# Cross-attention chain: the second attention written as one list of every engine's pieces, in place of a loop and a drain

## The chip, the cores and the metric

One core of one Trainium2 chip runs the kernel as a single program. The metric is device time in microseconds, the median of several executions. The engines are PE (matrix multiply), DVE (vector), ACT (scalar and activation), POOL (GpSimd) and SP, which only issues transfers. Each engine works through its own instructions in the order in which the program lists them, and waits in place when an instruction's data or buffer is not ready.

## The reference, cut to what matters

Thirty-two batches of 256 tokens with 256 features pass two layers:

```python
q, k, v = heads(tgt @ Wq.T), heads(mem @ Wk.T), heads(mem @ Wv.T)   # 16 heads
x = tgt + merge(softmax(q @ k.T / sqrt(dk)) @ v)[0]                 # batch 0's attention, added to all
norm_X   = layernorm(ctx, norm1_w, norm1_b)                         # memory
norm_F_L = layernorm(x, norm2_w, norm2_b)                           # queries
attended = softmax(norm_F_L @ norm_X.T * scale) @ norm_X            # first attention, per batch
h        = gelu(attended @ fc1_w.T + fc1_b)                         # 4 hidden values per token
cross    = h @ fc2_w.T + fc2_b
norm_c   = layernorm(cross, norm3_w, norm3_b)
self_att = softmax(norm_c @ norm_c.T * scale) @ norm_c              # second attention, per batch
out      = norm_F_L + gamma2 * (cross + gamma1 * self_att)
```

Only four hidden values per token enter `cross`, so the kernel never builds the 256-wide rows of the second attention. A token is a slot of at most 32 numbers: `v_sl` holds the four hidden values, a one, and later the weighted sums; `u_sl` and `t_sl` hold the normalised coefficients and their product with a small Gram matrix. Scores of the second attention are products over 32 rows.

## The kernel before, in words

The scheduler is off: the order of calls in the source is the order of the instructions on each engine, and buffers are handed out in that order.

Work is cut into 32 steps of one batch for the first attention (`first_step(s)`), in groups of four batches, g = 0 to 7. Groups of the second attention run behind, the first two already between the steps; the change begins where the steps end, at step 32. Steps 32 to 35 only finish the first attention of the last group.

For each group g the second attention consists of these pieces. A pair p is two batches; group g has the pairs 2g and 2g + 1.

- `third(k)`, for the two groups 2k and 2k + 1: a chain that alternates between POOL and DVE. `third_a` is a Gram product on POOL (L997), `third_b` a sum on DVE (L1007) and a product on POOL (L1009), `third_c` a sum on DVE (L1015), then on POOL a scaling, a power, a product and a second Gram product (L1017, L1019, L1022, L997), `third_d` a sum on DVE into `t_sl` (L1026). Ahead of `third(3)` stand `hide` (three small DVE operations) and `activate` (gelu on ACT).
- `turn_u(g)`: four transposes on PE and a copy of `u_sl` and `t_sl`; `turn_t(g)`: two transposes and a copy of `t_sl`; `turn_v(g)`: two and a copy of `v_sl`.
- A product by queries (pair p; `by_queries`) gives scores whose row maxima DVE takes (`scores_max`, L1153). A product by keys (`by_keys`) gives the transposed scores less the maxima, of which ACT takes the exponential (`weights`, L1165). `self_values(g)` sums over keys on PE (L354, named pu) and copies; `self_weighted(g)` transposes the sum (L1079); `divide(g)` divides on DVE (L1084, L1085) and writes `v_sl`. A product `to_output` (pair p) is added on DVE to `x_all` (`output`, L1175 for single banks, L1178 for a pair of banks), and SP stores 512 KB (L1179).
- `scale_skip(n)`: POOL multiplies batch n of `x_all` by a weight row (L764). The add of pair p needs batches 2p and 2p + 1 scaled. Batches 0 to 11 are scaled during the steps.

`pair_products` (L439) issues the eight products of 32 rows of each pair it is given. Two pairs, one even and one odd, use different row groups of PE, and their instructions are interleaved, two of the one and two of the other. The product of one pair needs two PSUM banks. There are three such places: `s0` and `s1`, each one buffer of two banks, and `et`, two buffers of one bank. Transposes and sums over keys use two buffers called `tp`.

In before a loop over j = 3 to 7 issues, in each round: the transposes of group j - 1, a pair block of queries 2j with keys 2j - 3, a block of output 2j - 6 with queries 2j + 1, the sums of group j - 2, a block of keys 2j - 2 with output 2j - 5, the division of group j - 2 and three or four scales. Behind it stands a drain of 42 lines for the last groups. Maxima use `s0`, keys use `s1`, outputs use `et`, until the drain.

Of the kernel before, what the change touches and what calls it, by code (L numbers as in the profile page):

```python
# [27 lines left out]
def tile_xattn_seq(  # L28
# [51 lines left out]
    def bank(tag, name):  # L80
        return ps.tile([P, NC, D], F32, tag=tag, name=name)
# [263 lines left out]
        copy(nxT_of[q][:, b], pt)  # L345

    def by_columns(psum, name, weights, moving, copy=nc.vector.tensor_copy, by_pairs=False):

        pg = psum(f"p{name}")
        order = [(kc, b) for kc in range(NC) for b in range(QB)]  # L350
        if by_pairs:
            order.sort(key=lambda at: at[1] // 2)
        for kc, b in order:
            nc.tensor.matmul(  # L354
                pg[SL * b : SL * (b + 1), 0, :],
                weights(kc, b),
                moving[:, b, kc, :],
                start=(kc == 0),
                stop=(kc == NC - 1),
            )  # L360
        t = wk.tile([P, D], F32, tag="col", name=f"col_{name}", bufs=3)
        copy(t, pg[:, 0, :])
        return t
# [639 lines left out]
        third[k] = times_gram(rows_of(k)[0], gram_m, NM, f"m{k}")  # L1003

    def third_b(k):
        vg = small.tile([P, TG, NM], F32, tag="vg3", name=f"vg3_{k}", bufs=2)
        nc.vector.tensor_reduce(vg, third.pop(k), AX.X, ALU.add)  # L1007
        vgv = small.tile([P, TG, NM], F32, tag="vgv3", name=f"vgv3_{k}", bufs=2)
        nc.gpsimd.tensor_mul(vgv, vg, rows_of(k)[0])  # L1009
        third[k] = vgv  # L1010

    def third_c(k):
        v5, u6, _ = rows_of(k)
        var = small.tile([P, TG], F32, tag="var3", name=f"var3_{k}", bufs=2)
        nc.vector.tensor_reduce(var, third.pop(k), AX.X, ALU.add)  # L1015
        ve = small.tile([P, TG], F32, tag="ve3", name=f"ve3_{k}", bufs=2)
        nc.gpsimd.tensor_scalar(ve, var, 0.0, EPS, ALU.max, ALU.add)  # L1017
        r3 = small.tile([P, TG, 1], F32, tag="r3", name=f"r3_{k}", bufs=2)
        nc.gpsimd.tensor_tensor(  # L1019
            r3.rearrange("p t o -> p (t o)"), ve, neg_half[:, 0:TG], ALU.pow  # L1020
        )
        nc.gpsimd.tensor_mul(u6[:, :, 0:NM], v5, r3.to_broadcast([P, TG, NM]))  # L1022
        third[k] = times_gram(u6, gram_k, NK, f"k{k}")
# [12 lines left out]
            )  # L1036

    def turn_u(g, copy=nc.scalar.copy):
        pt = bank("tp", f"pt_u{g}")
        slots_first(pt[:, 0, :], u_sl[:, g])  # L1040
        slots_first(pt[:, 1, :], t_sl[:, g])
        ut_of[g] = late.tile([P, NC, D], F32, tag="ut", name=f"ut_{g}", bufs=3)
        copy(ut_of[g], pt)

    def turn(what, sl, g, copy=nc.scalar.copy):

        pt = bank("tp", f"pt_{what}{g}")
        slots_first(pt[:, 0, :], sl[:, g])
        vt_of[what, g] = late.tile([P, D], F32, tag=f"{what}t", name=f"{what}t_{g}", bufs=2)
        copy(vt_of[what, g], pt[:, 0, :])  # L1050

    def turn_v(g, copy=nc.scalar.copy):
        turn("v", v_sl, g, copy)

    def turn_t(g, copy=nc.scalar.copy):
        turn("t", t_sl, g, copy)

    def by_queries(p, dst):
        ut = ut_of[p // 2]
# [8 lines left out]
    def self_values(g):  # L1068

        pvt_of[g] = by_columns(  # L1070
            tp_bank, f"u{g}", lambda kt, b: u_sl[:, g, kt, b, :], eT_of.pop(NQ + g), nc.scalar.copy
        )

    def self_weighted(g):

# [69 lines left out]
    ps2 = ctx.enter_context(tc.tile_pool(name="ps2", bufs=1, space=PSUM, reuse_waits="tile"))  # L1145

    def pair_bank(tag, name):
        t = ps2.tile([P, 2, NC, D], F32, tag=tag, name=name)
        return t, [t[:, i] for i in range(2)]

    def scores_max(p, sc):
        b = p % 2 * 2
        nc.vector.tensor_reduce(  # L1153
            t_sl[:, p // 2, :, b : b + 2, NK].rearrange("p t b -> p b t"),
            sc,
            AX.X,
            ALU.max,
            negate=True,
        )

    def weights(p, sc):
        if p % 2 == 0:
            eT_of[NQ + p // 2] = ld.tile([P, QB, NC, D], F32, tag="cq", name=f"eT2_{p // 2}")
        b = p % 2 * 2
        nc.scalar.activation(eT_of[NQ + p // 2][:, b : b + 2], sc, AF.Exp)  # L1165

    def out_banks(p):
        return [bank("et", f"po_{p}_{i}") for i in range(2)]

    def output(p, po):  # L1170

        if isinstance(po, list):
            for i in range(2):
                n = 2 * p + i
                nc.vector.tensor_add(x_all[:, n], po[i], x_all[:, n])  # L1175
        else:
            xs = x_all[:, 2 * p : 2 * p + 2]
            nc.vector.tensor_add(xs, po, xs)  # L1178
        nc.sync.dma_start(by_tokens(out[2 * p : 2 * p + 2]), x_all[:, 2 * p : 2 * p + 2])  # L1179


    first_step(B)
    sc, banks = pair_bank("s1", "sc1_2")
    pair_products(by_keys(2, banks))
    first_step(B + 1)
    weights(2, sc)
    pa = self_weighted(0)
    divide(0, pa)
    first_step(B + 2)
    third_d(2)  # L1190

    for j in range(3, NQ):


        turn_t(j - 1)
        if j == 3:
            turn_v(0, by_vector)
        sc0, b0 = pair_bank("s0", f"sc0_{2 * j}")
        sc1, b1 = pair_bank("s1", f"sc1_{2 * j - 3}")
        pair_products(by_queries(2 * j, b0), by_keys(2 * j - 3, b1))  # L1200
        scores_max(2 * j, sc0)
        if j > 3:
            turn_v(j - 3)
        weights(2 * j - 3, sc1)
        if j == 3:
            first_step(B + 3)
            hide(6, 8)
            activate(6)
            third_a(3)
        if j + 1 < NQ:  # L1210
            turn_u(j + 1)
        po = out_banks(2 * j - 6)
        sc0, b0 = pair_bank("s0", f"sc0_{2 * j + 1}")
        pair_products(to_output(2 * j - 6, po), by_queries(2 * j + 1, b0))
        if j < NQ - 1:
            output(2 * j - 6, po)
            scores_max(2 * j + 1, sc0)
        else:
            scores_max(2 * j + 1, sc0)
            output(2 * j - 6, po)  # L1220
        self_values(j - 2)
        if j == NQ - 1:
            break
        if j == 3:
            third_b(3)
        if j == 4:
            third_d(3)
        sc1, b1 = pair_bank("s1", f"sc1_{2 * j - 2}")
        po = out_banks(2 * j - 5)
        pair_products(by_keys(2 * j - 2, b1), to_output(2 * j - 5, po))  # L1230
        weights(2 * j - 2, sc1)
        pa = self_weighted(j - 2)
        output(2 * j - 5, po)
        divide(j - 2, pa)
        if j == 3:
            third_c(3)
        done = len(scaled_at) + max(3 * (j - 3), 4 * (j - 3) - 2)
        for n in range(done, min(done + (3 if j < 5 else 4), B)):
            scale_skip(n)
    for n in range(len(scaled_at) + 14, B):  # L1240
        scale_skip(n)


    g = NQ - 1
    sc1, b1 = pair_bank("s1", f"sc1_{2 * g - 2}")
    pair_products(by_keys(2 * g - 2, b1))
    weights(2 * g - 2, sc1)
    turn_t(g)
    sc0, b0 = pair_bank("s0", f"sc1_{2 * g - 1}")
    pair_products(by_keys(2 * g - 1, b0))  # L1250
    pa = self_weighted(g - 2)
    weights(2 * g - 1, sc0)
    divide(g - 2, pa)
    sc1, b1 = pair_bank("s1", f"sc1_{2 * g}")
    po = out_banks(2 * g - 5)
    pair_products(by_keys(2 * g, b1), to_output(2 * g - 5, po))
    output(2 * g - 5, po)
    turn_v(g - 2)
    weights(2 * g, sc1)
    self_values(g - 1)  # L1260
    sc0, b0 = pair_bank("s0", f"sc1_{2 * g + 1}")
    po = out_banks(2 * g - 4)
    pair_products(by_keys(2 * g + 1, b0), to_output(2 * g - 4, po))
    weights(2 * g + 1, sc0)
    pa = self_weighted(g - 1)
    divide(g - 1, pa)
    output(2 * g - 4, po)
    po1, b1 = pair_bank("s1", f"po_{2 * g - 3}")
    pair_products(to_output(2 * g - 3, b1))
    turn_v(g - 1)  # L1270
    output(2 * g - 3, po1)
    self_values(g)
    po = out_banks(2 * g - 2)
    po1, b1 = pair_bank("s0", f"po_{2 * g - 1}")
    pair_products(to_output(2 * g - 2, po), to_output(2 * g - 1, b1))
    pa = self_weighted(g)
    divide(g, pa)
    output(2 * g - 2, po)
    turn_v(g)
    output(2 * g - 1, po1)  # L1280
    po = out_banks(2 * g)
    po1, b1 = pair_bank("s1", f"po_{2 * g + 1}")
    pair_products(to_output(2 * g, po), to_output(2 * g + 1, b1))
    output(2 * g, po)
    output(2 * g + 1, po1)
# [1 line left out]
_INS = [  # L1287
    "x",
# [45 lines left out]
```

## Time and profile before

| what | value |
|---|---|
| median of 4 runs | 231.95 us (231.41 to 232.44) |
| profiled execution, its own time | 232.44 us |
| its span | 230.7 us |
| granted PE clock, mean | 0.985 |
| PE busy | 211.1 us, 92% |
| POOL busy | 174.5 us, 76% |
| DVE busy | 168.5 us, 73% |
| ACT busy | 148.3 us, 64% |
| bytes moved | 33.81 MB, of them 8.39 MB written |

Times in the profile run from the start of the span. The part that the change touches begins at about 173 us. A busy PE is a PE with at least one matrix multiply in flight by the profile's model, so a late start can hide inside busy time; the chain of waits, which splits time by what released what, shows it better. The page's list of the costliest groups gives the mean of one instruction; instructions that follow one another on an engine overlap a little, so that a run of them takes less than the sum of the means.

### The profile page before, as it was taken

The page shows a single profiled execution, that of the slowest core. Times are in us where ns is not written, and L with a number is a line of the kernel's source. Part 1 is how long each engine was busy: PE and PEld are TensorE (multiplying, and loading weights), DVE is VectorE, ACT ScalarE, POOL GpSimd, SP SyncE. Part 2 cuts the span into 40 slices and gives each one's busy share as a digit, 9 for nine tenths or more (in the row PEclk, how much of TensorE's full clock was granted, in tenths as well). Part 3 has the DMA queues.
Part 4 walks back from the last instruction along what each step waited for, and adds up shares of the span by engine and source line. Part 5 has one row for each costly group of instructions (what it writes and reads, how often), then busy time and mean ns, then how long its engine had stood idle before and what let it go on. Part 6 is the DMA issues. An engine that isn't in the chain of part 4 may idle for free.

```text
span 230.7 us, 4951 instructions
## 1 busy us (share of the span) xinstructions
PE 211.1 (92%) x1797; PEld 154.1 (67%) x1797; DVE 168.5 (73%) x409; ACT 148.3 (64%) x302; POOL 174.5 (76%) x274
## 2 busy tenths in 40 slices
PE   7999898898999989999998999989999998999950
PEld 6766555676787768697886887766775666655530
DVE  2797989899988748667677677686274977784681
ACT  2554968698988285966787968437846855545500
POOL 6067598576999999999978899997079479999300
PEclk9999999999999999999999999999999999999985
DMA  6889998999959964180730000000000224442277
GB/s 224 276 298 357 395 386 170 198 249 242 207 102 338 276 116 171 32 153 2 131 54 1 0 3 0 3 2 5 4 0 0 85 100 185 182 168 109 97 282 262
DMA packets 18038, 33.81 MB, mean 147 GB/s; under 512 B 1175, under 2 KB 2142, under 8 KB 18014
## 3 DMA queue, kind: packets, MB, share of 16 engines
q1 hardware_dynamic: 12974, 24.33, 29.5%
q0 software_dynamic: 3696, 7.34, 18.2%
q10 hardware_dynamic: 1344, 1.84, 2.3%
q8 instruction: 14, 0.23, 0.4%
q14 instruction: 10, 0.08, 0.1%
HBM read 17.73 MB, written 8.39 MB: 113 GB/s over the span
## 4 chain that ended last, share of the span: by engine, by line
PE 44%; POOL 23%; DVE 18%; DMA 4%; ACT 4%; issue 3%; DVEq 0%; POOLq 0%; ACTq 0%
PE sc L773 8%; PE sc L439 7%; POOL cq L307 6%; DMA x_all<-att 4%; POOL rs_b L227 4%; DVE st L211 4%; PE po L439 3%; PE pu L354 3%; POOL x_all L329 3%; DVE x_all L1175 2%; PE pt_e L202 2%; PE pv L354 2%; PE pt_x L202 2%; POOL rs_x L227 2%; PE ph L354 2%
## 5 line engine op out<-in xcount | busy, mean ns | idle before, releaser
L773 PE MATMUL sc<-nxT,nfT 128*128 128x256 f32 x256 | 62.4, 386 | 0.7 <-ACT nfT L755 0.7
L773 PEld LDWEIGHTS sc<-nxT,nfT 128*128 128x128 f32 x256 | 45.7, 190 | 12.1 <-issue 5.3
L764 POOL TENSOR_TENSOR x_all<-x_all,w_bc 128x512 f32<-128x512 f32 x32 | 39.7, 1286 | 0.0
L786 ACT ACTIVATE e<-sc,nm 128x256 f32<-128x256 f32 x64 | 26.9, 474 | 19.8 <-DVE nm L783 19.6
L783 DVE TENSOR_REDUCE nm<-sc 128x2 f32<-128x512 f32 x32 | 22.0, 687 | 22.1 <-PE sc L773 10.4
L755 ACT ACTIVATE nfT<-pt_x,bq,wq 128x256 f32<-128x256 f32 x64 | 33.3, 582 | 1.6 <-PE pt_x L202 1.5
L211 DVE BATCH_NORM_STATS2 st<-x_all 128x6 f32<-128x256 f32 x64 | 23.2, 412 | 1.8 <-DMA x_all<-att 1.7
L202 PE MATMUL pt_x<-ident,x_all 128*128 128x128 f32 x132 | 20.7, 278 | 1.5 <-POOL x_all L329 1.2
L202 PE MATMUL pt_c<-ident,cq 128*128 128x128 f32 x132 | 19.7, 276 | 2.2 <-ACT nfT L755 1.7
L211 DVE BATCH_NORM_STATS2 st<-cq 128x6 f32<-128x256 f32 x56 | 20.6, 412 | 0.0
L202 PE MATMUL pt_e<-ident,e 128*128 128x128 f32 x128 | 19.5, 275 | 0.6 <-ACT e L786 0.5
L1175 DVE TENSOR_TENSOR x_all<-po,x_all 128x512 f32<-128x512 f32 x26 | 16.7, 682 | 4.1 <-PE po L439 2.9
L307 POOL TENSOR_SCALAR cq<-cq,rs_b,nmr_b 128x256 f32<-128x256 f32 x32 | 19.4, 682 | 0.0
L795 ACT COPY eTq<-pt_e 128x512 f32<-128x512 f32 x32 | 18.5, 588 | 0.4 <-PE pt_e L202 0.4
L202 PEld LDWEIGHTS pt_x<-ident,x_all 128*128 128x128 f32 x132 | 15.4, 143 | 4.8 <-POOL x_all L329 2.4
L439 PE MATMUL po<-w_out,vt 32*128 32x256 f32 x128 | 17.5, 401 | 1.2 <-ACT vt L1050 1.0
L202 PEld LDWEIGHTS pt_e<-ident,e 128*128 128x128 f32 x128 | 15.4, 140 | 4.4 <-ACT e L786 1.6
L439 PE MATMUL sc<-tt,ut 32*128 32x256 f32 x128 | 17.6, 401 | 0.4 <-ACT eT L1165 0.4
L202 PEld LDWEIGHTS pt_c<-ident,cq 128*128 128x128 f32 x132 | 15.0, 141 | 3.9 <-ACT nfT L755 2.7
L1165 ACT ACTIVATE eT<-sc 128x1024 f32<-128x1024 f32 x14 | 14.4, 1027 | 4.6 <-PE sc L439 2.5
L345 DVE COPY nxT<-pt_c 128x512 f32<-128x512 f32 x23 | 15.6, 676 | 2.3 <-PE pt_c L202 2.3
L331 ACT ACTIVATE x_all<-x_all,nmr_b,rs_b 128x256 f32<-128x256 f32 x16 | 9.8, 618 | 10.9 <-POOL nmr_b L236 10.9
(215 smaller groups left out, 446.2 us busy)
## 6 DMA issues: line engine op xcount, KB each, us to landing
out_dram<-x_all SPq DMA_DIRECT2D x16, 512.0 KB
x_all<-att POOLq DMA_DIRECT2D x7, 1024.0 KB, 10.1
cq<-in_ctx_dram SPq DMA_DIRECT2D x6, 1024.0 KB
x_all<-in_x_dram SPq DMA_DIRECT2D x4, 1024.0 KB
x_all<-in_x_dram SPq DMA_DIRECT2D x1, 2048.0 KB
x_all<-in_x_dram SPq DMA_DIRECT2D x1, 1792.0 KB
cq<-in_ctx_dram ACTq DMA_DIRECT2D x1, 1024.0 KB
cq<-in_ctx_dram SPq DMA_DIRECT2D x1, 768.0 KB
```

Of the source, the lines that this page charges most:

```text
L202: nc.tensor.transpose(pt[:, dc, t * P : (t + 1) * P], src[:, t, dc * P : (dc + 1) * P], ident)
L211: nc.vector.bn_stats(st[:, t, :], src[:, t, :])
L307: nc.gpsimd.tensor_scalar(row, row, rs[:, i + t, :], nmr[:, i + t, :], ALU.mult, ALU.add)
L354: nc.tensor.matmul(pg[SL * b : SL * (b + 1), 0, :], weights(kc, b), moving[:, b, kc, :], start=(kc == 0), stop=(kc == NC - 1),)
L439: nc.tensor.matmul(dst[i][:, t, :], lhs[r : r + SL, t * P : (t + 1) * P], rhs[r : r + SL, :], start=True, stop=True,)
L755: nc.scalar.activation(nfT_of[n][:, dc, :], px[:, dc, :], AF.Identity, bias=bq[:, dc : dc + 1], scale=wq2[:, dc : dc + 1],)
L764: nc.gpsimd.tensor_mul(x_all[:, n], x_all[:, n], w2_bc.unsqueeze(1).to_broadcast([P, NC, D]))
L773: nc.tensor.matmul(sc[:, qt, :], nfT[:, dc, qt * P : (qt + 1) * P], nxT[:, dc, :], start=(dc == 0), stop=(dc == NC - 1),)
L783: nc.vector.tensor_reduce(nm, sc, AX.X, ALU.max, negate=True)
L786: nc.scalar.activation(e[:, qt, :], sc[:, qt, :], AF.Exp, bias=nm[:, qt : qt + 1])
L795: nc.scalar.copy(eT_of[q][:, b], turned(e_of.pop(n), "et", f"e_{n}"))
L1175: nc.vector.tensor_add(x_all[:, n], po[i], x_all[:, n])
```

## The change

The loop and the drain are replaced by one list of words, read from left to right. Each word is one engine's piece: transposes, their copy, a pair block, its maxima, exponentials or adds are words of their own, so that another piece can stand between a product and what drains it. Helpers are split for this (`by_columns` into `columns` and `copy_columns`, `turn_u` and `turn` into transposes and copy, `third_b` and `third_c` into their DVE and POOL halves).

A block names the place of each of its products (`q6@s1+q7@et`), so queries, keys and outputs may use any of `s0`, `s1` and `et`. In words: `q`, `k`, `o` products by queries, by keys and to the output; `max`, `exp`, `add` what drains them; `turn_x` transposes and `tT`, `uT`, `vT` their copies (`.v` on DVE, otherwise on ACT); `sums` and `col` the sums over keys and their copy; `turn_a` and `a` the transposes and the division; `pre`, `gelu`, `m`, `vg`, `vgv`, `var`, `r`, `t_k` the pieces of `third`; `scale` one scaling on POOL.

Keys of pair 3 are multiplied in one block with those of pair 2, between steps 33 and 34. All scales stand where the list puts them, from `scale12` on at its front. The copies of `turn_t` and `turn_v` have three buffers each instead of two. The pieces themselves and their sizes stay the same, except that a maximum or an exponential of a pair in `et` is two instructions of one bank, and an add of a pair in `s0` or `s1` one instruction of two banks.

```diff
-    def turn(what, sl, g, copy=nc.scalar.copy):
+    def turned_slots(what, g):
         pt = bank("tp", f"pt_{what}{g}")
-        slots_first(pt[:, 0, :], sl[:, g])
-        vt_of[what, g] = late.tile([P, D], F32, tag=f"{what}t", name=f"{what}t_{g}", bufs=2)
+        slots_first(pt[:, 0, :], {"v": v_sl, "t": t_sl}[what][:, g])
+        return pt
+
+    def copy_slots(what, g, pt, copy):
+        vt_of[what, g] = late.tile([P, D], F32, tag=f"{what}t", name=f"{what}t_{g}", bufs=3)
         copy(vt_of[what, g], pt[:, 0, :])
...
     def pair_bank(tag, name):
+        if tag == "et":
+            banks = [bank("et", f"{name}_{i}") for i in range(2)]
+            return banks, [(i, i + 1, banks[i].unsqueeze(1)) for i in range(2)]
         t = ps2.tile([P, 2, NC, D], F32, tag=tag, name=name)
-        return t, [t[:, i] for i in range(2)]
+        return [t[:, i] for i in range(2)], [(0, 2, t)]
...
+    def products(*todo):
+        by = {"q": by_queries, "k": by_keys, "o": to_output}
+        args = []
+        for what, p, tag in todo:
+            banks, held[what, p] = pair_bank(tag, f"{what}_{p}")
+            args.append(by[what](p, banks))
+        pair_products(*args)
...
     first_step(B)
-    sc, banks = pair_bank("s1", "sc1_2")
-    pair_products(by_keys(2, banks))
-    first_step(B + 1)
-    weights(2, sc)
     pa = self_weighted(0)
     divide(0, pa)
+    first_step(B + 1)
+    products(("k", 2, "s1"), ("k", 3, "s0"))
+    weights(2, held.pop(("k", 2)))
+    weights(3, held.pop(("k", 3)))
     first_step(B + 2)
-    third_d(2)
-
-    for j in range(3, NQ):
...
-    output(2 * g, po)
-    output(2 * g + 1, po1)
+    order = """
+    scale12 q6@s1+q7@et t_k2 turn_t2 max6 scale13 turn_u4 tT2 turn_n7 uT4.v k4@s0+k5@s1
+    scale14 n7 max7 sums1 exp4 scale15 turn_u5 exp5 col1.v q8@s0+q9@et pre6 scale16 uT5
+    gelu6 sums2 max8 scale17 max9 q11@s1+q10@s0 m3 max11 turn_t4 scale18 col2 tT4
+    turn_a2 turn_v0 vg3 k9@et+k8@s1 vT0 a2 vgv3 max10 scale19 turn_t3 exp9 turn_a1 var3
+    exp8 a1 r3 o1@s0+o0@et tT3.v turn_v1 add1 sums4 vT1 add0 turn_v2 col4 o3@s0+k6@s1
+    vT2 turn_a4 add3 exp6 k7@et scale20 a4 o4@s1+o5@s0 exp7 t_k3 scale21 turn_t5 add4
+    turn_u7 tT5 turn_u6 uT7 add5 scale22 uT6 q15@s1+k10@et scale23 q12@s0 max15 exp10
+    scale24 max12 q13@et+q14@s1 sums3 scale25 max13 turn_v4 col3 max14 scale26
+    o2@s0+k11@et vT4 turn_t6 add2 exp11 scale27 turn_t7 o9@s1 tT6 tT7 scale28 turn_a3
+    k14@s0+k15@et a3 add9 scale29 turn_v3 exp15 sums5 vT3.v scale30 exp14 o7@et+k12@s1
+    col5.v scale31 turn_a5 add7 exp12 sums7 o6@s1+k13@s0 col7.v a5 turn_a7 add6 exp13
+    turn_v5 o8@et vT5 a7 o10@s1+o11@s0 add8 sums6 add11 turn_v7 col6 add10 vT7 turn_a6
+    o14@s0+o15@et a6 add14 turn_v6 vT6 add15 o12@s1+o13@s0 add12 add13
+    """
...
+    for word in order.split():
+        if "@" in word:
+            todo = [part.split("@") for part in word.split("+")]
+            products(*((name[0], int(name[1:]), tag) for name, tag in todo))
+            continue
+        word, *by = word.split(".")
+        name = word.rstrip("0123456789")
+        steps[name](int(word[len(name) :]), *([by_vector] if by else []))
```

More of the change, by code (lines that the diff above doesn't have):

```diff
@@ L347, in by_columns, with columns @@
     def by_columns(psum, name, weights, moving, copy=nc.vector.tensor_copy, by_pairs=False):
+        return copy_columns(columns(psum, name, weights, moving, by_pairs), name, copy)
+    def columns(psum, name, weights, moving, by_pairs=False):
         pg = psum(f"p{name}")
@@ L360, in by_columns, with copy_columns @@
             )
+        return pg
+    def copy_columns(pg, name, copy):
         t = wk.tile([P, D], F32, tag="col", name=f"col_{name}", bufs=3)
@@ L1005, in third_b, with third_vg, third_vgv @@
     def third_b(k):
+        third_vg(k)
+        third_vgv(k)
+    def third_vg(k):
         vg = small.tile([P, TG, NM], F32, tag="vg3", name=f"vg3_{k}", bufs=2)
         nc.vector.tensor_reduce(vg, third.pop(k), AX.X, ALU.add)
+        third[k] = vg
+    def third_vgv(k):
+        vg = third.pop(k)
         vgv = small.tile([P, TG, NM], F32, tag="vgv3", name=f"vgv3_{k}", bufs=2)
@@ L1012, in third_c, with third_var, third_r @@
     def third_c(k):
-        v5, u6, _ = rows_of(k)
+        third_var(k)
+        third_r(k)
+    def third_var(k):
         var = small.tile([P, TG], F32, tag="var3", name=f"var3_{k}", bufs=2)
         nc.vector.tensor_reduce(var, third.pop(k), AX.X, ALU.add)
+        third[k] = var
+    def third_r(k):
+        v5, u6, _ = rows_of(k)
+        var = third.pop(k)
         ve = small.tile([P, TG], F32, tag="ve3", name=f"ve3_{k}", bufs=2)
@@ L1038, in turn_u, with turned_u @@
     def turn_u(g, copy=nc.scalar.copy):
+        copy_u(g, turned_u(g), copy)
+    def turned_u(g):
         pt = bank("tp", f"pt_u{g}")
@@ L1041, in turn_u, with copy_u @@
         slots_first(pt[:, 1, :], t_sl[:, g])
+        return pt
+    def copy_u(g, pt, copy):
         ut_of[g] = late.tile([P, NC, D], F32, tag="ut", name=f"ut_{g}", bufs=3)
         copy(ut_of[g], pt)
-    def turn(what, sl, g, copy=nc.scalar.copy):
+    def turned_slots(what, g):
         pt = bank("tp", f"pt_{what}{g}")
-        slots_first(pt[:, 0, :], sl[:, g])
-        vt_of[what, g] = late.tile([P, D], F32, tag=f"{what}t", name=f"{what}t_{g}", bufs=2)
+        slots_first(pt[:, 0, :], {"v": v_sl, "t": t_sl}[what][:, g])
+        return pt
+    def copy_slots(what, g, pt, copy):
+        vt_of[what, g] = late.tile([P, D], F32, tag=f"{what}t", name=f"{what}t_{g}", bufs=3)
         copy(vt_of[what, g], pt[:, 0, :])
-    def turn_v(g, copy=nc.scalar.copy):
-        turn("v", v_sl, g, copy)
     def turn_t(g, copy=nc.scalar.copy):
-        turn("t", t_sl, g, copy)
+        copy_slots("t", g, turned_slots("t", g), copy)
     def by_queries(p, dst):
@@ L1072, in self_values, with self_sums @@
         )
+    def self_sums(g):
+        return columns(tp_bank, f"u{g}", lambda kt, b: u_sl[:, g, kt, b, :], eT_of.pop(NQ + g))
     def self_weighted(g):
@@ L1147, in pair_bank, with scores_max @@
     def pair_bank(tag, name):
+        if tag == "et":
+            banks = [bank("et", f"{name}_{i}") for i in range(2)]
+            return banks, [(i, i + 1, banks[i].unsqueeze(1)) for i in range(2)]
         t = ps2.tile([P, 2, NC, D], F32, tag=tag, name=name)
-        return t, [t[:, i] for i in range(2)]
-    def scores_max(p, sc):
+        return [t[:, i] for i in range(2)], [(0, 2, t)]
+    def scores_max(p, pieces):
         b = p % 2 * 2
[L1153 to L1177, printed above, removed]
+        for lo, hi, sc in pieces:
+            nc.vector.tensor_reduce(
+                t_sl[:, p // 2, :, b + lo : b + hi, NK].rearrange("p t b -> p b t"),
+                sc,
+                AX.X,
+                ALU.max,
+                negate=True,
+            )
@@ L1178, in output, with weights @@
+    def weights(p, pieces):
+        g, b = p // 2, p % 2 * 2
+        if NQ + g not in eT_of:
+            eT_of[NQ + g] = ld.tile([P, QB, NC, D], F32, tag="cq", name=f"eT2_{g}")
+        for lo, hi, sc in pieces:
+            nc.scalar.activation(eT_of[NQ + g][:, b + lo : b + hi], sc, AF.Exp)
+    def output(p, pieces):
+        for lo, hi, po in pieces:
+            xs = x_all[:, 2 * p + lo : 2 * p + hi]
             nc.vector.tensor_add(xs, po, xs)
         nc.sync.dma_start(by_tokens(out[2 * p : 2 * p + 2]), x_all[:, 2 * p : 2 * p + 2])
+    held = {}
@@ L1189, in tile_xattn_seq @@
+    weights(2, held.pop(("k", 2)))
+    weights(3, held.pop(("k", 3)))
     first_step(B + 2)
-    third_d(2)
-    for j in range(3, NQ):
[L1195 to L1283, printed above, removed]
-    output(2 * g, po)
-    output(2 * g + 1, po1)
+    order = """
+    scale12 q6@s1+q7@et t_k2 turn_t2 max6 scale13 turn_u4 tT2 turn_n7 uT4.v k4@s0+k5@s1
@@ new lines, in tile_xattn_seq, with turn_a, sums, col @@
+    """
+    def turn_a(g):
+        held["a", g] = self_weighted(g)
+    def sums(g):
+        held["sums", g] = self_sums(g)
+    def col(g, copy=nc.scalar.copy):
+        pvt_of[g] = copy_columns(held.pop(("sums", g)), f"u{g}", copy)
+    def turn_n(g):
+        held["n", g] = tokens_first(tp_bank, col_of.pop(g), f"v{g}")
+    def n(g):
+        nc.vector.tensor_copy(n_all[:, g], held.pop(("n", g))[:, :, :, 0:NM])
+    steps = {
+        "turn_t": lambda g: held.update({("t", g): turned_slots("t", g)}),
+        "turn_v": lambda g: held.update({("v", g): turned_slots("v", g)}),
+        "turn_u": lambda g: held.update({("u", g): turned_u(g)}),
+        "tT": lambda g, copy=nc.scalar.copy: copy_slots("t", g, held.pop(("t", g)), copy),
+        "vT": lambda g, copy=nc.scalar.copy: copy_slots("v", g, held.pop(("v", g)), copy),
+        "uT": lambda g, copy=nc.scalar.copy: copy_u(g, held.pop(("u", g)), copy),
+        "max": lambda p: scores_max(p, held.pop(("q", p))),
+        "exp": lambda p: weights(p, held.pop(("k", p))),
+        "add": lambda p: output(p, held.pop(("o", p))),
+        "a": lambda g: divide(g, held.pop(("a", g))),
+        "sums": sums,
+        "col": col,
+        "turn_a": turn_a,
+        "turn_n": turn_n,
+        "n": n,
+        "pre": lambda lo: hide(lo, lo + 2),
+        "gelu": activate,
+        "m": third_a,
+        "vg": third_vg,
+        "vgv": third_vgv,
+        "var": third_var,
+        "r": third_r,
+        "t_k": third_d,
+        "scale": scale_skip,
+    }
```

## The prediction

> **What bounds the kernel now.** I read the page first (PE 92% busy, so nothing else can be shortened for long), then the chain of waits from 173 us, where the two programs part, then the timeline and half-microsecond windows of the same stretch. The timeline, start, duration, engine and, in brackets, the idle time before and its releaser:
>
> ```profile
> 177.23 2.51 POOL L764 TENSOR_TENSOR x_all<-x_all,w_bc 128x512 f32<-128x512 f32 x2
> ...
> 181.68 1.03 POOL L997 TENSOR_TENSOR w_m<-v_sl,gram_m 128x400 f32<-128x400 f32 x1 [1.94 <-ACT v_sl L983]
> ...
> 190.81 24.66 POOL L764 TENSOR_TENSOR x_all<-x_all,w_bc 128x512 f32<-128x512 f32 x20
> ```
> ```profile
> 201.93 1.29 DVE L1175 TENSOR_TENSOR x_all<-po,x_all 128x512 f32<-128x512 f32 x2 [1.18 <-POOL x_all L764]
> ...
> 203.63 0.77 PE L439 MATMUL po<-w_out,vt 32*128 32x256 f32 x3
> ...
> 206.19 0.44 PE L1034 MATMUL pt_v<-ident,v_sl 128*128 128x128 f32 x2
> 206.72 0.37 ACT L1050 COPY vt<-pt_v 128x256 f32<-128x256 f32 x1 [1.26 <-PE pt_v L1034]
> 207.14 0.48 PE L439 MATMUL po<-w_out,vt 32*128 32x256 f32 x2 [0.52 <-ACT vt L1050]
> ```
> PE waits in small pieces: an output product follows its own transpose and copy at once (206.19 to 207.14); a pair block of two products takes 1.46 us (202.87 to 204.33), since o7 needs the et banks that o6 filled one block earlier, and the add that empties them (201.93, 1.29 us) lies between. The bracket puts that add down to POOL, but it begins 0.06 us behind the end of o6's block (201.87), and its scales were done at 193.3: the releaser is PE. POOL was idle and then ran all twenty scales in a row, 1.233 us each.
>
> The chain has the clean prices (start, length, what):
>
> ```profile
> 216.04 0.37 PE pt_a L1079 x2
> 216.41 1.06 PE po L439 x8
> 217.47 0.37 PE pt_v L1034 x2
> 217.84 1.00 PE pu L354 x16
> 218.85 1.07 PE po L439 x16
> ```
> A pair block is 1.07, a lone product 1.06, sums over keys 1.00, two transposes 0.37 (0.22 right behind other transposes: pt_t at 198.20), four 0.44. From the windows, the end (columns: length; PE, PEld, DVE, ACT, POOL busy with counts; clock; DMA share; GB/s):
>
> ```profile
> 220.00:221.00 1.00, 0.37 (x3) 0.17 (x3) 0.64 (x3) 0.00 (x0) 0.00 (x0) 1.00 1.00 379
> 221.00:222.00 1.00, 0.48 (x3) 0.24 (x4) 1.00 (x3) 0.37 (x1) 0.00 (x0) 1.00 0.82 311
> 222.00:223.00 1.00, 1.00 (x16) 0.84 (x16) 1.00 (x1) 0.00 (x0) 0.00 (x0) 1.00 0.00 0
> 223.00:224.00 1.00, 0.25 (x5) 0.00 (x0) 1.00 (x3) 0.00 (x0) 0.00 (x0) 0.85 0.69 254
> ```
> The last product ends at 223.25, the last add at 225.49; the span ends at 230.7, 5.2 us behind that add, while the last four stores (0.52 MB each) run back to back in 5.5 us, 1.38 each.
>
> **The change, part by part.** *PE work.* Both programs hold the same 40 products from 173 us on (18 pair blocks and 4 alone), the same sums and transposes. So the gain can only be in waits. From 190.71 the kernel before does 12 pair blocks (12.84), 3 lone products (3.18), 5 sums (5.00), 13 transposes at 0.37 and 3 at 0.22 (5.47) and two fours (0.88): 27.37 us of work in 32.54 (190.71 to 223.25). Its waits there are 5.17.
>
> *POOL and DVE up to o1.* Scales 12 to 17 now go straight behind scale 11, ahead of m3 (the gram product of third(3)). The first such product, w_k of third(2), ends at 177.28; eight scales at 1.233 end at 187.1; m3 takes 1.03, to 188.1. In before it ran at 181.68, as soon as gelu was done. On DVE, vg3 now waits for it, though DVE is done with max11 at about 186.75 (by the same prices PE ends k2+k3 at 176.1, q6+q7 at 178.3, k4+k5 at 180.7, q8+q9 at 183.2, q11+q10 at 185.5). Queued behind vg3 are a2, max10, var3 and a1. PE waits for two of them: vg3 0.50, a2 0.44, max10 1.13 bring 190.3, and o1+o0 needs max10's bank s0. So o1+o0 starts at 190.35. PE, free from 188.3 except for one transpose pair, loses about 1.7 us here; because of this anchor, what happens earlier (k3 early beside k2, the table switch for gelu, 1.28 each way) costs nothing unless it is over 1.4 us late on DVE or 0.7 on ACT (exp9 ends at 189.65). If that cover goes, every microsecond counts in full.
>
> *PE from o1.* Remaining: 12 pair blocks (12.84), 4 lone products (4.24), 5 sums (5.00), 12 transposes at 0.37 and 3 at 0.22 (5.10), two fours (0.88): 28.06, which would end at 218.41 (before, likewise, 190.71 + 27.37 = 218.08: the list is 0.33 behind here). I followed the list by hand with DVE max and add at 1.13 to 1.2 (1.25 for two single banks), exp 1.03 (1.1 for two: four take 2.1 in before), copies 0.37 and 0.59, divide 0.44. Waits left:
> - q15+k10 for uT7 (transposes 0.60, hop 0.08, copy 0.59, hop 0.05, against 0.88 of PE work): 0.44
> - q13+q14 for exp10 and max15 (1.28 against lone q12, 1.06): 0.22
> - turn_a6 for col6 (0.49 against 0.37): 0.12
> - o14+o15 for vT7 (0.97 against 0.71): 0.26
> - o12+o13 for vT6 (0.96 against 0.37), 0.59, then o13 for add14's bank, 0.27
> - four blocks that begin from a wait, 1.17 as at 200.70 and not 1.07: 0.40
>
> That is 2.30. All other blocks find vT, tT and their bank ready, by 0.1 us at the tightest (o2+k11 behind max13, k13 behind exp12), since three slots (s0, s1, et) take turns and a transpose's copy has a block of PE work over it. Hops between engines that I have not listed I take from a stretch that looks streamed: 212.31 to 219.85 lasts 7.54, its pieces sum to 7.39, so 2%, 0.56 on 28.06. Between ends of 0 and the 2.87 that would bring before's 5.17 again, I take 0.56, the nearest row. The last product then ends at 218.41 + 2.30 + 0.56 = 221.3, 2.0 earlier than 223.25.
>
> *POOL afterwards.* var3 at 190.5 and scale 19 (190.9) release r3 (0.28, 2.92, 0.34, 1.33 with hops: 196.0); t_k3 fits on DVE at 196.0 to 196.8, ahead of turn_u7. Scales 20 to 31 end at 210.8 instead of 215.5; the adds that need them (10 to 15) are all later.
>
> *Tail and stores.* The order at the end is again four adds behind a divide: last product 221.3, add12 and add13 end at 223.5 (before: 2.24 behind the product). Stores start some ten microseconds later, at about 192 instead of 182.4; 16 at 1.38 are 22.1 us in 33, so the queue is no bound until the last seven, which come every 1.13 to 1.2 and pile up 0.1 more than before. SP has nothing else queued. The Trainium skill, DMA: Bandwidth & Descriptors, section Specifications, gives about 358 GB/s from HBM per core; by that a store would take an estimated 1.46 us and seven of them 0.6 us more. The windows here show 375 to 391, so I keep 1.38. End: 223.5 + 5.2 + 0.05 = 228.75.
>
> **Sum.** Span 228.75 against 230.7: 1.95 less. The profiled execution took 232.44, 1.74 more than its span; the median of the four times is 231.95, so the change gives 231.95 - 1.95 = 230.0.
>
> **Rivals.**
> *Clock.* PE's granted clock is 1.00 until 223.5 to 224.0, where it drops to 0.70 and then 0.50. From 220.5 to 224.0 PE was busy 1.82 of 3.5 us (52%); 41 to 44 (2.21 of 3.0, 74%) kept 1.00. In my list, 188.0 to 191.5 has about 1.8 of 3.5. If that halves the clock for as long again, PE loses 1.75: 231.75, no change. Against it: the 52% of before includes the kernel's end. The Trainium skill (TensorE: Matmul & The Clock Gate, Part 1) would need a whole idle window of some 3.4 us and so foresees no drop; its section on a second HAM failure mode, psum-queue depth-cycling, speaks against this change, saying that short idle times between bank groups can make the clock swing. The trace's drop 0.45 us behind the last matmul fits the first rule badly. Chance 0.10.
>
> *The waits only move.* DVE's load is unchanged and a list in fixed order stalls elsewhere. Then waits stay at 5.17 and the 0.33 is lost: 231.95 + 0.33 = 232.3. For it: the new DVE stall at vg3; against it: the cover worked out above. Chance 0.08.
>
> *Slower: pair blocks lose their overlap.* Two products share 1.07 only if both banks are free; else the late one runs alone. Before's eight blocks from 191.3 to 208.4 took 2.02, 1.24, 1.33, 1.41, 1.17, 1.46, 1.27 and 1.30, mean 1.40. If the twelve behind o1 do the same in place of about 1.10, that is 3.6: 233.6. It decides for slower from a mean of 1.36, where (1.36 - 1.10) x 12 = 3.1 exceeds the 1.95 gained and the 1.16 of 0.5%. For it: the tight places have 0.1 us; against it: before's late et had only the 1.00 of sums over it, where an add and its hops need 1.39; in the list a bank used twice running behind o1 has 1.37 or more over it (sums and a transpose pair), except at the last block. Chance 0.18.
>
> **How the numbers follow.** The forecast has 0.64, with its own range 228.6 (the 0.56 nil, 0.8 of the 2.30 gone) to 231.0 (hops three times the 0.56, rounded down); 0.04 of it lies above 230.8, that is within 0.5% (about what a measurement of this kernel can tell from no change, 1.16 us). Faster 0.60; same 0.04 + 0.10 + 0.08 = 0.22; slower 0.18. The range leaves out the slower rival: 228.6 to 232.7.
>
> **What would show it.** Right: w_m of third(3) on POOL near 188 and vg at once behind it, a PE gap there, o1 near 190.4; PE almost without gaps from there; scales done near 211; last product near 221.3; end 5.2 behind the last add. Wrong: pair blocks over 1.3 on average, a granted clock below 1.00 before 220, PE gaps at blocks I called covered, or o1 starting later than 191.

## The result and the profile after

| | before | after |
|---|---|---|
| median | 232.13 us (66 runs) | 230.96 us (40 runs) |
| ratio to before | | 0.9961, 95% interval 0.9949 to 0.9974 |
| profiled execution, its own time | 232.44 us | 230.69 us |
| its span | 230.7 us | 228.9 us |
| granted PE clock, mean | 0.985 | 0.987 |

The change gained 1.17 us by the medians where 1.95 was forecast. The ratio compares means and gives 0.39%, that is 0.90 us; its interval excludes 1, so the change is faster, though by less than the 0.5% up to which the prediction spoke of the same time. The two spans differ by 1.8, more than the medians, and the reason matters for everything below: executions drift against each other ahead of the changed part. A mark that all versions share, the start of POOL's power in third(2) (`r`), lies at 172.52 in before and at 171.95 in after; a second profile of the kernel before has it at 171.83, and all ten profiles have it between 171.30 and 172.52. So lengths below run from that mark. From it to the start of the last output product it is 49.32 us in before, and 48.07 in after: 1.25 less. To compare with the forecast's places, add 0.57 to those of after.

In the new lines L445 is the pair products, L770 the scale, L986 and L988 the two `pre` operations on DVE, L989 gelu, L1003 the Gram products, L1017 vg, L1189 the maxima, L1202 the exponentials, L1207 the adds. The timeline of POOL in after (start, duration, engine, what, count):

```profile
176.69 9.86 POOL L770 TENSOR_TENSOR x_all<-x_all,w_bc 128x512 f32<-128x512 f32 x8
186.52 1.01 POOL L1003 TENSOR_TENSOR w_m<-v_sl,gram_m 128x400 f32<-128x400 f32 x1
...
195.33 14.81 POOL L770 TENSOR_TENSOR x_all<-x_all,w_bc 128x512 f32<-128x512 f32 x12
```

The scales now come as the list says: eight in a row with w_m behind them, two singly (left out above), and twelve more that end at 210.14. The timeline of all engines around o1+o0, in after:

```profile
181.95 1.01 DVE L986 TENSOR_TENSOR pre<-n_all,rd_f 128x64 f32<-128x64 f32 x1
183.06 1.13 DVE L988 TENSOR_TENSOR pre<-pre,fc1b_all 128x64 f32<-128x64 f32 x1
184.12 3.54 DVE L1189 TENSOR_REDUCE t_sl<-q 128x4 f32<-128x1024 f32 x4
185.38 1.13 PE L445 MATMUL q<-ut 32*128 32x256 f32 x12 [0.83 <-DVE t_sl L1189]
187.58 0.56 DVE L1017 TENSOR_REDUCE vg<-w_m 128x80 f32<-128x400 f32 x1
189.04 1.28 ACT L1202 ACT_TABLE_LOAD   x1 [0.72 <-PE k L445]
189.67 0.77 PE L445 MATMUL o<-w_out,vt 32*128 32x256 f32 x4
190.34 2.00 ACT L1202 ACTIVATE eT<-k 128x512 f32<-128x512 f32 x3
190.99 1.61 PE L445 MATMUL o<-w_out,vt 32*128 32x256 f32 x12 [0.55 <-ACT eT L1202]
```

Two things here are not in the prediction. The load of the exponential's table (1.28 us) stands between the product k9+k8 and its exponential, with ACT idle for 0.72 ahead of it; the block o1+o0, cut in two by it, lasts from 189.67 to 192.60, 2.93 us where 1.17 was forecast. And the two small `pre` operations take 1.01 and 1.13 us; in before they took 0.22 and 0.23, while POOL stood idle (179.74 to 181.68). The timeline of before, with its own load of the exponential's table:

```profile
180.60 0.22 DVE L980 TENSOR_TENSOR pre<-n_all,rd_f 128x64 f32<-128x64 f32 x1
180.93 0.23 DVE L982 TENSOR_TENSOR pre<-pre,fc1b_all 128x64 f32<-128x64 f32 x1
...
182.82 1.28 ACT L1165 ACT_TABLE_LOAD   x1
```

The chain of waits of after names the load and both `pre` operations (start, length, what):

```profile
181.95 1.02 DVE pre L986
183.06 1.13 DVE pre L988
184.19 2.34 DVE t_sl L1189 x3
...
186.58 0.45 PE pt_t L1056 x2
...
187.92 1.11 PE k L445 x16
...
189.04 1.28 ACT L1202
190.34 0.61 ACT eT L1202
190.99 1.61 PE o L445 x12
```

The end, in windows of a microsecond (columns as in the prediction):

```profile
220.00:221.00 1.00, 0.98 (x14) 0.89 (x16) 1.00 (x3) 0.00 (x0) 0.00 (x0) 1.00 1.01 381
221.00:222.00 1.00, 0.52 (x8) 0.12 (x2) 1.00 (x2) 0.00 (x0) 0.00 (x0) 1.00 1.02 375
222.00:223.00 1.00, 0.00 (x0) 0.00 (x0) 1.00 (x2) 0.00 (x0) 0.00 (x0) 0.92 1.03 377
```

The last product ends at 221.52, the last add at 223.79 and the span 5.1 us behind that. The clock stays at 1.00 up to the last product.

### The profile page after: what moved, and what is told of

The parts are those of the page before. It is cut to its first block, busy times and chain, and to the rows that moved or that the text cites. A ratio compares the mean times of both kernels' runs of the same rounds, so it can differ in the third digit from the quotient of the medians.

```text
span 228.9 us, 4945 instructions
## 1 busy us (share of the span) xinstructions
PE 209.1 (91%) x1797; PEld 152.3 (67%) x1797; DVE 171.5 (75%) x408; ACT 146.9 (64%) x302; POOL 174.1 (76%) x274
## 4 chain that ended last, share of the span: by engine, by line
PE 58%; POOL 15%; DVE 12%; ACT 6%; DMA 3%; issue 3%; DVEq 1%; ACTq 0%; POOLq 0%
PE sc L779 15%; PE o L445 5%; PE pt_e L202 3%; POOL cq L307 3%; PE pt_x L202 3%; PE pt_c L202 3%; DMA wv_nat<-in_L_xattn_Wv_dram 3%; PE pu L357 3%; POOL rs_b L227 3%; PE k L445 3%; DVE st L211 2%; PE sc L445 2%; PE ph L357 2%; PE pv L357 2%; PE sk L445 2%
## 5 line engine op out<-in xcount | busy, mean ns | idle before, releaser
L770 POOL TENSOR_TENSOR x_all<-x_all,w_bc 128x512 f32<-128x512 f32 x32 | 39.7, 1267 | 0.0
L1207 DVE TENSOR_TENSOR x_all<-o,x_all 128x1024 f32<-128x1024 f32 (+1 forms) x20 | 19.2, 1005 | 4.0 <-PE o L445 2.0
L1202 ACT ACTIVATE eT<-k 128x512 f32<-128x512 f32 (+1 forms) x19 | 14.2, 798 | 7.8 <-PE k L445 7.8
L445 PE MATMUL o<-w_out,vt 32*128 32x256 f32 x128 | 14.0, 401 | 1.2 <-ACT eT L1202 0.5
L227 POOL TENSOR_TENSOR rs_x<-ve_x,neg_half 128x2 f32<-128x2 f32 (+2 forms) x9 | 9.4, 1044 | 4.1 <-DVE ve_x L226 3.1
```

What stands on the lines that cost most here:

```text
L227: nc.gpsimd.tensor_tensor(rs.rearrange("p n o -> p (n o)"), ve.rearrange("p n o -> p (n o)"), neg_half[:, 0:n], ALU.pow,)
L445: nc.tensor.matmul(dst[i][:, t, :], lhs[r : r + SL, t * P : (t + 1) * P], rhs[r : r + SL, :], start=True, stop=True,)
L770: nc.gpsimd.tensor_mul(x_all[:, n], x_all[:, n], w2_bc.unsqueeze(1).to_broadcast([P, NC, D]))
```

## The experiments

Theory A: the table load for exp9, which runs only when k9+k8 is done, costs about 1.3 us at o1+o0. Theory B: POOL's scales slow DVE's `pre` operations, and with them everything on DVE up to max10, which releases o1+o0. Rivals: the load is hidden under max10 anyway; the lateness of m3 behind six scales (12 to 17), not the `pre` operations, sets max10; or the early keys of pair 3 moved the wait.

The walk can be told by three lengths per run: from the mark to the start of o1+o0, that block itself, and from its end to the start of the last product. All in us. The runs come from more than one chip, so the ratio is always to the kernel before on the same chip.

| run | time | ratio and 95% interval | mark to o1+o0 | o1+o0 | then to the last product | mark to the last product |
|---|---|---|---|---|---|---|
| after | 230.96 | 0.9961 (0.9949 to 0.9974) | 17.72 | 2.93 | 27.42 | 48.07 |
| e10, key 3 not early | 231.09 | 0.9967 (0.9946 to 0.9989) | 17.69 | 2.92 | 27.42 | 48.03 |
| e1, table early | 229.74 | 0.9923 (0.9896 to 0.9950) | 17.69 | 1.66 | 27.40 | 46.75 |
| e4, scales later | 229.53 | 0.9916 (0.9887 to 0.9945) | 16.58 | 2.93 | 27.42 | 46.93 |
| e7, both, two scales back | 229.33 | 0.9889 (0.9854 to 0.9925) | 17.70 | 1.66 | 27.41 | 46.77 |
| e5, both | 228.28 | 0.9855 (0.9826 to 0.9884) | 16.58 | 1.66 | 27.40 | 45.64 |
| e9, both, keys 2 and 3 in the hole | 228.23 | 0.9841 (0.9807 to 0.9874) | 16.86 | 1.65 | 27.42 | 45.93 |
| before | 232.13 | | | | | 49.32 |
| e6, before again | 231.76, one execution | | | | | 49.32 |
| e8, before with the table early | 231.57 | 0.9986 (0.9966 to 1.0006) | | | | 49.31 |

**e1: the exponential's table loaded early.** One exponential of a single column, whose operand is ready from the start, right behind the last gelu:

```diff
-    gelu6 sums2 max8 scale17 ...
+    gelu6 early_exp6 sums2 max8 scale17 ...
+    def early_exp(g):
+        t = small.tile([P, 1], F32, tag="tiny", name=f"tiny_{g}", bufs=1)
+        nc.scalar.activation(t, neg_half[:, 0:1], AF.Exp)
```

> The changed kernel with one more ACT instruction, an Exp of one column right behind gelu6, so that the exp table is loaded there and not with exp9. Theory A (the late table load ate the gain): in the changed kernel the load begins only behind k9+k8 (189.04) and o1+o0 takes 2.93 us (189.67 to 192.60) waiting for exp9's banks. Here the load stands at about 184.5, exp9 begins within 0.1 us of k9+k8's end, o1+o0 takes at most 1.4 us and ends 1.4 to 1.7 us earlier, and the time falls by 1.0 to 1.6 us below the changed kernel's 230.96, to about 229.7. Rival (the waits only move: DVE or the store queue would have set the end anyway): o1+o0 gets shorter, the time stays within 0.3 us of 230.96.

Measured: 229.74 us. The timeline has the load at another place and the block in one piece:

```profile
184.86 1.28 ACT L1270 ACT_TABLE_LOAD   x1
...
190.03 1.66 PE L445 MATMUL o<-w_out,vt 32*128 32x256 f32 x16
```

The block starts where it did (17.69 against 17.72) and is 1.27 shorter; the whole is 1.32 shorter. The load was not hidden, and Theory A has its size. That size rests on the lengths: by the ratios, the intervals of e1 and of after still touch. The block is longer than the 1.4 expected here, though exp9 now begins at once behind k9+k8 (189.42).

**e4: scales 14 to 31 behind the Gram product.** Only POOL's order differs: scales 14 to 16 move behind m3, 17 to 31 behind r3.

```diff
-    scale14 n7 ... exp4 scale15 ... pre6 scale16 uT5 ... max8 scale17 ... m3 max11 ... scale18 ...
+    n7 ... exp4 ... pre6 uT5 ... max8 ... m3 scale14 max11 ... a2 scale15 ... turn_a1 scale16 var3
+    exp8 a1 r3 scale17 ... scale31 ...
```

> The changed kernel with POOL's order alone changed: scales 14 to 16 behind m3, 17 to 31 behind r3. Theory B (POOL's scales hold up DVE's two small additions of pre6): in the changed kernel L986 and L988 take 1.01 and 1.13 us beside a scale, 0.22 and 0.23 in the kernel before with POOL idle; max8 begins 1.7 us late and PE idles 0.83 at q10. Here both take 0.22 to 0.3, max8 begins 1.5 us earlier, k9+k8 ends 1.3 to 1.5 us earlier, the table load with it, and the time falls by 1.0 to 1.5 us, to about 229.7. Theory A alone expects the same fall only if k9+k8 ends earlier. Rival (the two additions are slow for another reason, such as their operands' place): they stay at 1.0, nothing moves, within 0.3 us of 230.96.

Measured: 229.53 us. DVE's timeline:

```profile
181.62 0.23 DVE L986 TENSOR_TENSOR pre<-n_all,rd_f 128x64 f32<-128x64 f32 x1
181.95 0.22 DVE L988 TENSOR_TENSOR pre<-pre,fc1b_all 128x64 f32<-128x64 f32 x1
182.63 3.55 DVE L1189 TENSOR_REDUCE t_sl<-q 128x4 f32<-128x1024 f32 x4 [0.46 <-PE q L445]
186.10 0.56 DVE L1017 TENSOR_REDUCE vg<-w_m 128x80 f32<-128x400 f32 x1
```

With POOL idle, `pre` has its old price, the maxima now wait for PE's product and not the reverse, and o1+o0 starts 1.14 earlier by the mark (16.58 against 17.72). The 1.3 to 1.5 expected for the end of k9+k8 is missed: max8 begins 1.15 earlier and k9+k8 ends 1.14 earlier, since PE's product now sets the start of max8. The block is still 2.93 long, as the load is still in it: the two causes don't touch each other. That all later scales run as one row costs nothing: the last length is 27.42, as in after.

**e5: both mends.** The edits of e1 and e4 together.

> Both edits. A and B together: o1+o0 ends about 2.5 to 3 us earlier than in the changed kernel (near 189.8), and, if PE streams behind it as it does there, the time falls by 2.0 to 2.8 us, to about 228.4. If only one of the two matters the time is that of the better one. Rival (waits move): 230.7 or more.

Measured: 228.28 us, ratio 0.9855. By the mark, 48.07 becomes 45.64; 1.32 and 1.14 sum to 2.46, and 2.43 was measured; o1+o0 ends 2.41 earlier, just short of the 2.5 expected. This version beats both kernels.

**e6: the kernel before, once more.** No edit.

> The kernel before once more, unchanged, for a second profile. The forecast subtracted spans of one profiled execution each. If the difference of the spans (230.7 against 228.9, 1.8 us) is larger than that of the medians (about 0.9 to 1.2) because the stretch before step 33 differs from execution to execution, then the stretch from the transposes of step 31 to the end (56.2 us in the first profile, 55.1 in the changed kernel's) repeats within 0.3 us here, and the start of it lies within 1 us of 174.5.

Measured: the span was 229.98 in place of 230.7, but from the mark to its end 58.15 and 58.18. The part behind 172 us repeats within 0.03 in these two executions; what differs between them lies ahead of it. This is why the lengths in the table can be read to a few hundredths where the times can't.

**e7: two scales put back ahead of m3.** From e5, `scale14` and `scale15` stand beside `pre6` again; six scales (10 to 15) instead of after's eight (10 to 17) lie ahead of m3, and the early exponential stays.

```diff
-    n7 max7 sums1 exp4 turn_u5 ... m3 scale14 max11 ... a2 scale15 vgv3 ...
+    scale14 n7 max7 sums1 exp4 scale15 turn_u5 ... m3 max11 ... a2 vgv3 ...
```

> The both-mends kernel with scales 14 and 15 put back ahead of the Gram product m3, where the changed kernel has them, so that they run beside DVE's pre6; everything else, the tiny early exponential included, stays. Theory (POOL's scales slow DVE's two-input pre6): the two pre operations take about 1.0 and 1.1 us again in place of 0.22 and 0.23, max8 begins about 1.5 us later than in the both-mends kernel, o1+o0 starts about 1 us later, and the time is 0.6 to 1.3 us above 228.28: about 229.2. Rival (only the lateness of m3 behind six scales cost time): with two scales ahead of it m3 is still early enough, the pre operations don't matter, and the time is within 0.3 us of 228.28.

Measured: 229.33 us. From its timeline:

```profile
182.50 0.99 DVE L986 TENSOR_TENSOR pre<-n_all,rd_f 128x64 f32<-128x64 f32 x1
183.60 1.13 DVE L988 TENSOR_TENSOR pre<-pre,fc1b_all 128x64 f32<-128x64 f32 x1
185.10 1.01 POOL L1003 TENSOR_TENSOR w_m<-v_sl,gram_m 128x400 f32<-128x400 f32 x1 [0.45 <-ACT v_sl L989]
188.11 0.56 DVE L1017 TENSOR_REDUCE vg<-w_m 128x80 f32<-128x400 f32 x1
```

w_m ends at 186.11, 2.0 us ahead of vg, so m3 is not late at all here. Still all of e4's gain is gone (17.70 to o1+o0, 1.12 more than e5): DVE's wait beside a scale is enough to cost it, and the rival that put it down to m3's place alone falls. What m3's place would cost without that wait no run shows. In after w_m ends 15.58 behind the mark, and in e4 vg begins at 14.49, so w_m alone would hold vg by an estimated 1.1, about as much: e4 had to move the scales away from both. Against e1 only POOL's order differs (six scales ahead of m3 in place of eight, the late ones behind r3), and the lengths are the same within 0.02.

**e8: the early exponential in the kernel before.** The same tiny exponential behind gelu of third(3), in the old order.

> The kernel before with the same tiny exponential right behind the gelu of third(3), nothing else. In the kernel before, the table load for the next exponential stands at 182.82 and PE waits 0.44 us near there, before a stretch whose end is set by the chain of third(3) and by DVE. If the exposed load is a cost that the list alone brought, this changes the time by less than 0.3 us (231.8 on that chip). If the kernel before pays for it as well, it gets up to 0.7 us faster (231.1), and so much of the gain of the mend is not the list's.

Measured: 231.57 us, and 49.31 by the mark against 49.32. In before that load stood at 182.82. Moved forward, it lets PE's products behind it come up to 0.34 earlier by the mark (the block at 187.15 in before begins 14.63 behind the mark, here 14.29). But the transposes of `v_sl` after them wait for DVE's division, 0.85 in place of 0.57, and begin where they did (20.81 against 20.80): the load was covered there. The 1.3 us of Theory A are a cost that the list brought.

**e9: keys 2 and 3 in PE's hole.** From e5, the block is moved ahead of step 33.

```diff
     first_step(B)
+    products(("k", 2, "s1"), ("k", 3, "s0"))
     pa = self_weighted(0)
     divide(0, pa)
     first_step(B + 1)
-    products(("k", 2, "s1"), ("k", 3, "s0"))
```

> The both-mends kernel with the block of keys 2 and 3 issued where the kernel before had keys 2 alone, ahead of step 33 and of the division of group 0, in a hole of about 0.67 us that PE has near 173 us. If the stretch up to o1+o0 is still set by PE's order there, everything behind comes 0.3 to 0.65 us earlier: 227.6 to 228.0. If DVE or POOL set that stretch, the time stays at 228.28 within 0.3.

Measured: 228.23 us, by the mark 0.29 longer than e5 (16.86 against 16.58 to o1+o0). The time alone would say that PE's order near 173 us does not set the stretch; the timeline says otherwise. The block takes 1.61 us there, the transposes of step 33 come behind it, ACT copies them later, and the product that reads the copy (named pv) takes 1.79 in place of 1.07. So q6+q7 begin 0.28 later by the mark (5.00 against 4.72), and o1+o0 is later by the same 0.28. The hole only moved, and this run does not show what filling it would be worth.

**e10: the third pair's weights not early.** The changed kernel with keys 2 alone ahead of step 33, then queries 6 with keys 3, then queries 7 alone.

```diff
-    products(("k", 2, "s1"), ("k", 3, "s0"))
...
-    scale12 q6@s1+q7@et t_k2 turn_t2 max6 scale13 ...
+    scale12 q6@s1+k3@s0 t_k2 turn_t2 max6 exp3 q7@et scale13 ...
```

> The changed kernel with the third pair's weights not early: keys 2 alone at the place that the kernel before gives them, then queries 6 with keys 3, then queries 7 alone. PE has one lone product more at 173 and one pair block less early. If the early keys of pair 3 bring something, this is 0.5 to 1.0 us slower than the changed kernel's 230.96 (231.5 to 232.0). If they are hidden by the wait for the exponential's table and by DVE, as my prediction's anchor at o1+o0 said, the time is 230.96 within 0.3, since keys 2 in the hole gives back what the lone product costs.

Measured: 231.09 us, and 48.03 by the mark against 48.07. The early weights are worth nothing in this list, as the prediction had it. What hides them in the trace is the scale beside `pre`: `pre` begins 0.66 later than in after by the mark (10.66 against 10.00) and ends at the same place (12.20 against 12.24). This run also shows how `pre` waits; two scales of POOL, then the two operations on DVE, from its timeline:

```profile
182.03 2.49 POOL L770 TENSOR_TENSOR x_all<-x_all,w_bc 128x512 f32<-128x512 f32 x2
...
183.07 0.32 DVE L986 TENSOR_TENSOR pre<-n_all,rd_f 128x64 f32<-128x64 f32 x1
183.49 1.12 DVE L988 TENSOR_TENSOR pre<-pre,fc1b_all 128x64 f32<-128x64 f32 x1
```

One of these scales lasts 1.26, so the first ends at about 183.3 and the second at 184.52. `pre` ends at 183.39 and at 184.61: each operation ends about 0.09 behind the scale in which it began, whether that leaves it 0.32 or 1.12.

## Why the prediction was right and wrong

**What held.** The same work on PE, so a gain in waits only. POOL's price (eight scales forecast at 9.86, 9.86 measured), w_m's end (187.53 + 0.57 = 188.10 against 188.1), vg at once behind it, max10 as the releaser of o1+o0 and its start (189.67 + 0.57 = 190.24 against 190.35), the end of all scales (210.14 + 0.57 = 210.7 against 210.8), 7.4 us from the last product to the end of the span (7.45 forecast). That the early keys bring nothing: e10. Pair blocks share their time as costed: o3+k6 takes 1.07 (194.27 to 195.34), o7+k12 the same (209.78 to 210.85).

The start of o1+o0 was right in part by luck. The prediction had it set by w_m, with DVE done 1.35 earlier. In after w_m does end at 187.53, but DVE's maxima, late by `pre`, end at 187.66 (184.12 + 3.54), so both hold vg. In e7 w_m ended 2.0 us ahead of vg, and o1+o0 began at the same place.

**Where it failed: the covers ahead of o1+o0.** The prediction said that the block would begin at 190.35 and take a block's usual time, unless something was over 1.4 us late on DVE or 0.7 on ACT, with exp9 ending at 189.65. Both covers were used up:

- On ACT, the load costs 1.30 us between k9+k8 and exp9. The prediction knew of the table switch (1.28 each way) but let it stand among the things that "happen earlier", as if it ran as soon as ACT was free. In the trace it runs only when exp9's data are there. This is the step that failed: an instruction on the path put down as one beside it. Worth 1.32 (after against e1).
- On DVE, the two `pre` operations were counted at before's 0.22, measured with POOL idle, though the change puts scales beside them. They cost 1.01 + 1.13 - 0.45 = 1.69. They ate the margin of 1.4 (DVE comes to vg only as w_m ends), made q11+q10 wait 0.83 for max8, and by the chain of waits held the transposes turn_t4, which need max9, until 186.58; so k9+k8 and exp9 came later.

By these lines exp9 ends at about 190.34 + 1.1 = 191.44, or 192.0 with the 0.57: 2.4 late, against a cover of 0.7. That leaves 1.7, and the block was 1.76 longer than forecast.

**What was too dear.** Behind the block the forecast had 27.0 of work and 2.76 of waits (2.30 named and 0.56 of hops, less the 0.10 named for the block itself). After needs 28.92 from 192.60 to 221.52, so 1.93 of waits, 0.83 less. And this part is rigid: to the start of the last product it took 27.40 to 27.42 in all seven runs of the list, whatever came before it.

**The sum.** -0.11 for the start, +1.76 for the block, -0.83 behind it: +0.82, and the last product ended at 221.52 + 0.57 = 222.09 against 221.27 (221.3 rounded). Of the 1.95 forecast, 223.25 - 222.09 = 1.16 came by the end of that product, 1.25 by its start (it takes 1.50 against 1.41), 1.17 by the medians. Had the load been early as in e1, the gain would have been 49.32 - 46.75 = 2.57.

**The rivals.** The clock did not halve: the granted clock was 1.00 until the last product. The waits did not only move: from the start of o1+o0 to the end of the last product after takes 31.85 for 28.06 of work, so 3.79 of waits, the load and its block among them, against before's 5.17. The pair blocks did not lose their overlap; only o1+o0, q13+q14 (2.45 together with the lone q12 by the chain of waits, where 1.06 + 1.07 is the clean price) and the last block (1.50) lost part of it. The mean of 1.40 that the prediction had for before counts into its first block the wait of 0.57 for DVE's division that ends at 193.32; without it the mean is 1.33. The rule against the change that the prediction weighed (the Trainium skill, TensorE: Matmul & The Clock Gate, A second HAM failure mode: psum-queue depth-cycling) did not show here. A rule that bore on it was missed: the Trainium skill, SBUF — State Buffer, section Who interferes with whom, says that a DVE instruction with two SBUF inputs contends with a GpSimd instruction that reads SBUF, and that the port pair which the two share is an exclusive lock. The traces agree: 0.22 with POOL idle, 0.32 to 1.13 beside a scale, each time until that scale ended. DVE's reciprocal just ahead of `pre`, with one input, took 0.24 beside a scale in after and 0.25 with POOL idle in before.

**What stays open.** Why o1+o0 takes 1.66 and not 1.07 even with both mends was not tried; by e5's timeline exp9 begins at 188.47, only 0.61 ahead of the block, so o0's second bank comes free inside it. What the lateness of w_m costs by itself was not run, nor `pre` without it. What makes executions differ by up to 1.2 us ahead of the mark was not looked for.

## What to carry to other kernels

When a list moves an instruction, price it beside its new neighbours, not its old: a 0.22 us vector operation became 1.1 us because another engine now ran over it. Of a cover, ask not only how much there is but which instructions could eat it, table loads first: a load belongs to the activation behind it and may run only when that one's data are there; a tiny activation of the same function, with an operand that is always ready, pulls it forward (1.32 us here). Before comparing two executions, find a mark that they share, since what lies ahead of it can differ by as much as the change is worth.

## What the runs showed of the hardware

- A table load can wait for the data of its activation. For exp9 the load began 0.01 to 0.02 us behind the end of k9+k8 in after, e4 and e10, each time with ACT idle 0.72 ahead of it. It is not always so: the load for gelu ran at 182.63 in after, right behind ACT's copy, and gelu itself then waited 0.32 for `pre`. In after's trace gelu itself carries its wait for DVE, while the first exponential of exp9 carries one for POOL and none for PE. That the wait for PE stood on the load in its place would explain the difference, but it is not shown: the trace keeps no waits of a load.
- A vector operation with both inputs in SBUF that begins beside a POOL scale ends 0.07 to 0.10 us behind the end of that scale (after, e7 and e10), so a 0.22 us operation costs 0.32 to 1.13 us, by where in the scale it begins.
